# A macaron layer on one NeuronCore: the attention's output projection moved behind the heads, by two levels of seven products, with operands kept in DRAM

## The chip, the cores and the metric

The kernel runs on one core of one Trainium2 chip, in float32 throughout. The metric is the device time of one execution, in microseconds, of which the median over several runs is given. A profile of one execution is read beside it; its span runs from the first to the last instruction, and its own device time is a little more than the span.

## The reference

The input x has 1024 tokens (4 sequences of 256) of 512 numbers. Three blocks follow each other, each on the normalised x and added to x:

```python
x = x + 0.5 * _L0_ffn_ref(_layernorm(x), A, B, Wr)      # experts
x = x + _L0_attn_ref(_layernorm(x), wq, wkv, wo)        # 32 heads, causal
x = x + 0.5 * _L0_ffn_ref(_layernorm(x), A, B, Wr)      # the same experts again
```

The experts are 64 pairs of rank 16: h = x Aᵀ (512 to 1024), each h times its token's gate (softmax over the 16 largest of 64 scores), then h B (1024 to 512). The attention makes q, k and v of 128 numbers per head, softmax of the causal scores, and at the end multiplies the heads' outputs, 1024 tokens by 4096, with wo (4096 by 512). That last product is the output projection, and it is what changes place and form.

## The kernel before

**Seven products.** All large products go by Strassen's scheme in Winograd's form: a product of two 2×2 block matrices by 7 block products instead of 8, with sums of blocks ahead (`left_sums`, `right_sums`: four additions each) and seven additions of results behind. `seven` walks the products in the order M1, M2, M6, M5, M7, M3, M4; they share three PSUM banks, several products are added into one bank by TensorE, and each bank is read between two of them. For q, k and v two levels are nested (49 block products instead of 64): `xop` holds the 7×7 blocks of the normalised x, `two_levels` makes the 7×7 blocks of the weights on POOL, and `make_qk` and `v_stages` run one outer product or two at a time as a stage of seven inner ones.

**Order.** The heads are worked in 16 groups `p` of two. While group p attends, the q and k of group p+1 and a part of v are made. A group has 8 units, each a (head, sequence): `probs` (scores, mask, softmax) and, one unit later, `attend` (three transposes, then probabilities times v). The strings in `UNITS` (L994) say which step is taken between: q a q/k step, v a v step, o a step of the output projection, b the second half of `attend`. TensorE takes its instructions in the order a scheduler writes down[...].

**The output projection before.** It has one level and one group: K is two heads of 128, the tokens two halves of 512, the 512 outputs two halves of 256. `out_sums` makes three sums of 512 columns of the group's attention output (and one in place) on POOL, `sums_o` the four sums of wo's blocks on POOL, `project(p, u)` the seven products for a quarter of the tokens, each as two matmuls of 256 columns (L879), and reads the accumulators straight into x, seven times 512 columns (L891). The projection of group p-1 runs among the units of group p. For each group that is 28 matmuls and 14 reads.

**The second experts' layer** loads A and B again at the end and makes their block sums again on POOL (`load_experts(ctx, "f2", ...)`, L1057); it pairs token blocks t and t+4 (L1081).

**q and k.** For p > 0, `make_qk` runs four stages: (M1, M5), (M2, M6), (M7, M3), (M4), most of them two outer products wide, 512 columns; the parts are put together by adds on POOL (`done`, L711). `t3` and `t4` (L552, L555) turn weight block M1 into M7 and M2 into M4, in place, when the former use is over.

Of the kernel before, what the change touches and what calls it, by code (L numbers as in the profile page):

```python
# [13 lines left out]
P = 128  # L14
# [18 lines left out]
def macaron_kernel(  # L33
# [14 lines left out]
    small = ctx.enter_context(tc.tile_pool(name="small", bufs=4))  # L48
    xscope = ctx.enter_context(ExitStack())
# [30 lines left out]


    mask = const.tile([P, 3, P], F32, tag="mask", name="mask")
    nc.gpsimd.memset(mask, 0.0)
    for blk in (0, 2):
        nc.gpsimd.affine_select(
            out=mask[:, blk, :],
            in_=mask[:, blk, :],
            compare_op=ALU.is_ge,
            fill=MASKED,
            base=0,  # L90
            pattern=[[-1, P]],
            channel_multiplier=1,
        )
    mask_f = mask.rearrange("p b k -> p (b k)")

# [89 lines left out]
    def right_sums(eng, t, b11, b12, b21, b22, late=None, pinned=False):  # L185


        late = late or eng
        first = eng.tensor_tensor(b12, b12, b11, ALU.subtract)  # L189
        if pinned:  # L190
            tc.keep_in_program_order(first)
        eng.tensor_tensor(t[0], b22, b12, ALU.subtract)  # L192
        late.tensor_tensor(t[1], t[0], b11, ALU.subtract)
        late.tensor_tensor(t[2], b21, t[0], ALU.subtract)
        return {"M1": b11, "M2": b21, "M3": b22, "M4": t[2], "M5": b12, "M6": t[0], "M7": t[1]}
# [17 lines left out]
    def load_experts(scope, name, side, eng, between=None):  # L213
# [8 lines left out]
        a_v = a_t.rearrange("(c p) k -> p c k", p=P)  # L222
        b_v = b_t.rearrange("(c p) d -> p c d", p=P)

        def a_block(k, n):
            return slice(2 * k, 2 * k + 2), slice(512 * n, 512 * n + 512)

        def b_block(k, n):
            return slice(4 * k, 4 * k + 4), slice(256 * n, 256 * n + 256)

        for i, kn in enumerate(((0, 0), (1, 0), (1, 1), (0, 1))):
            c, e = a_block(*kn)
            nc.sync.dma_start(a_sb[:, c, e], a_v[:, c, e])
            if between is not None and i % 2:
                between(i // 2)
        for k in range(2):
# [4 lines left out]
        b_of = [b_sb[(slice(None), *b_block(*kn))] for kn in every]  # L241
        return (
            lambda: right_sums(eng, [at[:, i] for i in range(3)], *a_of, late=nc.gpsimd),
            lambda: right_sums(nc.gpsimd, [bt[:, i] for i in range(3)], *b_of),
        )

    def ffn(name, pairs, a_sums, b_sums, after, late, aside=None):


        with ExitStack() as scope:  # L250
# [165 lines left out]
            take(tokens, 1)  # L416
            if late:
                second = prepare(pairs[1])
                take(second, 1)
# [54 lines left out]
    OUTER = {"M1": 0, "M2": 1, "M7": 2, "M4": 3, "M5": 4, "M6": 5, "M3": 6}  # L474
    INNER = {"M1": 0, "M2": 1, "M7": 2, "M4": 3, "M5": 4, "M6": 5, "M3": 6}
    xop = xpool.tile([P, 7, 7, S], F32, tag="xop", name="xop")


    early = xop[:, 5:7, 6]

    def inner_sums(lo, hi, eng, between=None):
        o = slice(lo, hi)
        blocks = [xop[:, o, i] for i in range(4)]
        if lo == 0:
            blocks[2] = early
        left_sums(eng, [xop[:, o, i] for i in (4, 5, 6, 2)], *blocks, pinned=lo > 0, between=between)

    def last_outer():

        for of, i in ((early[:, 1], 2), (xop[:, 1, 3], 3)):  # L490
            tc.keep_in_program_order(
                nc.gpsimd.tensor_tensor(xop[:, 6, i], of, xop[:, 5, i], ALU.subtract)
            )

    def norm_pair(work, pair):
# [4 lines left out]
        where = [xop[:, k, 4:6, :].rearrange("p a s -> p (a s)") for k in (5, 6)]  # L500
        tokens = normed(work, pair, "a", where)
        yield
        for i, xn in enumerate(tokens):
            cols = slice(i * P, (i + 1) * P)
            pt = turned_x(xn, f"a_{pair[i]}").rearrange("p (o c) k -> p o c k", o=2)
            a11, a12, s3, a22, s1, s2, _ = (xop[:, k, sl, cols] for k in range(7))
            if half:
                nc.scalar.copy(a22, pt[:, 1])
                if a:
                    nc.vector.tensor_tensor(s3[:, 0], early[:, 0, cols], pt[:, 0, 0], ALU.subtract)  # L510
                    nc.vector.tensor_tensor(s3[:, 1], a11[:, 1], pt[:, 0, 1], ALU.subtract)
                else:
                    nc.vector.tensor_tensor(s3, a11, pt[:, 0], ALU.subtract)
                nc.vector.tensor_tensor(s2, pt[:, 1], s3, ALU.subtract)
                nc.vector.tensor_tensor(s1, a22, pt[:, 0], ALU.add)
            elif a:
                nc.scalar.copy(early[:, :, cols], pt[:, :, 0])
                nc.scalar.copy(xop[:, 0:2, 3, cols], pt[:, :, 1])
            else:
                nc.scalar.copy(xop[:, 0:2, sl, cols], pt)  # L520
        if half and not a:
            nc.vector.tensor_tensor(xop[:, 6, sl], xop[:, 1, sl], xop[:, 5, sl], ALU.subtract)
        elif a and not half:
            inner_sums(0, 2, nc.vector)

    raw, rights, outs, turns = {}, {}, {}, {}

    def load_o(p):

        w = opool.tile([P, HG, 512], F32, tag="w", name=f"wo_{p}")  # L530
        nc.sync.dma_start(w, wo_v[:, p * HG : (p + 1) * HG, :])
        raw["o", p] = w

    def sums_o(p):
        w = raw["o", p]
        t = opool.tile([P, 3, 256], F32, tag="t", name=f"to_{p}")
        b = [w[:, k, n * 256 : (n + 1) * 256] for k in range(2) for n in range(2)]
        rights["o", p] = right_sums(nc.gpsimd, [t[:, i, :] for i in range(3)], *b, pinned=p == 0)

    def two_levels(pool, bufs, name, blocks, pinned):  # L540
# [5 lines left out]
            for m in ("M1", "M5", "M2", "M3", "M6")  # L546
# [8 lines left out]
        def t4():  # L555
            return nc.gpsimd.tensor_tensor(t["M2"], t["M2"], t["M6"], ALU.subtract)

        def sums(pinned=pinned):
            plain = {m: v[:, 0:4] for m, v in t.items()}
            first = nc.gpsimd.tensor_tensor(plain["M5"], plain["M5"], plain["M1"], ALU.subtract)  # L560
            if pinned:
                tc.keep_in_program_order(first)
            nc.gpsimd.tensor_tensor(plain["M6"], plain["M3"], plain["M5"], ALU.subtract)
            right = {
                m: right_sums(
                    nc.gpsimd, [v[:, i] for i in range(4, 7)], *(v[:, i] for i in range(4))
                )
                for m, v in t.items()
            }
            right["M7"], right["M4"] = right["M1"], right["M2"]  # L570
            return right, t3, t4
# [3 lines left out]
    def load_qk(p):  # L575

        if p < NG:
            rights["qk", p] = two_levels(
                qkpool,
                6,  # L580
# [7 lines left out]
    def load_v(k):  # L588

        if 2 * k < NG:  # L590
            raw["v", k] = two_levels(
                vpool,
                5,
# [11 lines left out]
    with ExitStack() as scope:  # L605
# [7 lines left out]
            *experts,  # L613
# [4 lines left out]
        take(first_layer, 2)  # L618
# [7 lines left out]

    qkpool = right_pool(ctx, "wqk")
    hold = right_pool(ctx, "hold")
    opool = right_pool(ctx, "wo")
    attention = ExitStack()  # L630
    work = right_pool(attention, "work")
    pairs = right_pool(attention, "pairs")

# [8 lines left out]
    def make_qk(p):  # L642
        if p >= NG:
            return
        right, t3, t4 = rights["qk", p]
# [6 lines left out]
        def stage(ms, read, name):  # L652
            def product(n, ps, first):
                for i, m in enumerate(ms):
# [3 lines left out]
                        rhs=xop[:, OUTER[m], INNER[n]],  # L658
# [10 lines left out]
        def fresh(blocks):  # L669
            def read(r, ps):  # L670
                to = part(blocks, r)
                if READS[r][2]:
                    nc.vector.tensor_tensor(to, to, ps, ALU.add)
                else:
                    nc.scalar.copy(to, ps)
# [3 lines left out]
        def branch(blocks, into=None, of=slice(1, 2)):  # L679

            base = of

            def read(r, ps):
                to = part(blocks, r)
                of = to if READS[r][2] else part(base, r).to_broadcast(to.shape)
                nc.vector.tensor_tensor(to, of, ps, ALU.add)  # L686
                done(r, into)

            return read

        def onto(blocks, into=None):
            def read(r, ps):
                to = part(blocks, r)
                of = ps if ps.shape == to.shape else ps.to_broadcast(to.shape)
                nc.vector.tensor_tensor(to, to, of, ALU.add)  # L695
                done(r, into)

            return read

        def m47(r, ps):  # L700

            both, one, two, base = (part(slice(*k), r) for k in ((1, 3), (1, 2), (2, 3), (3, 4)))
            if READS[r][2]:
                nc.vector.tensor_tensor(both, both, ps, ALU.add)
            else:
                nc.scalar.copy(one, ps[:, 0:1])
                nc.vector.tensor_tensor(two, base, ps[:, 1:2], ALU.add)
            if r in LAST:
                nc.gpsimd.tensor_tensor(one, one, two, ALU.add)

        def done(r, into):  # L711

            if into is not None and r in LAST:
                to, a, b = (part(slice(k, k + 1), r) for k in (into, 1, 2))
                nc.gpsimd.tensor_tensor(to, a, b, ALU.add)  # L715


        if p > 0:
            yield from stage(("M1", "M5"), fresh(slice(1, 3)), "a")
            t3()  # L720
            yield from stage(("M2", "M6"), branch(slice(0, 2), 3), "b")
            t4()
        else:
            turns["qk"] = t3, t4

            yield from stage(("M1",), fresh(slice(3, 4)), "m")
            yield from stage(("M2",), branch(slice(0, 1), of=slice(3, 4)), "n")
            yield from stage(("M6",), onto(slice(3, 4)), "o")
            yield from stage(("M4", "M7"), m47, "r")
            yield from stage(("M5",), onto(slice(2, 4)), "s")  # L730
            load_qk(p + 1)
            yield from stage(("M3",), onto(slice(3, 4)), "u")
            return
# [389 lines left out]
```

## Time and profile before

| | us |
|---|---|
| median of 3 runs | 1177.11 (1176.92 to 1177.27) |
| the profiled execution's own time | 1176.84 |
| its span | 1175.1 |
| TensorE (PE) busy | 1162.9 |
| weight loads (PEld) busy | 1001.7 |
| VectorE (DVE) busy | 733.4 |
| POOL (GpSimd) busy | 681.5 |
| ScalarE (ACT) busy | 490.8 |
| moved by DMA | 47.46 MB |

Busy times are sums over the span. A matmul's record is longer than its share of the engine, since matmuls overlap: pace is read from the starts of successive rows. A float32 matmul leaves two records, so a count of 8 records is four matmuls. The transposes leave one.

### The profile page before, as it was taken

The numbers are of one execution on the slowest core, as the hardware profiler recorded it, in microseconds if no ns is written. First come the engines' busy times: TensorE is split into PE (matmuls) and PEld (weight loads), VectorE is DVE, ScalarE is ACT, GpSimd is POOL, SyncE is SP. The second block draws the span as 40 slices with busy tenths as digits, with TensorE's granted clock in tenths as the row PEclk, the third lists the DMA queues.
The fourth block names the chain that finished last, engine by engine and source line by source line (L and its number), as shares of the span: only waits on it lengthen the run. The fifth ranks groups of instructions, "written<-read, shape, count | busy, mean of one in ns | idle before, by whom it ended". The sixth has DMA issues, their size and how long they took to land.

```text
span 1175.1 us, 18545 instructions
## 1 busy us (share of the span) xinstructions
PE 1162.9 (99%) x6492; PEld 1001.7 (85%) x6492; DVE 733.4 (62%) x1927; ACT 490.8 (42%) x1365; POOL 681.5 (58%) x942
## 2 busy tenths in 40 slices
PE   8999999999999999999999999999999999999998
PEld 5677889999999989898989898989898988875767
DVE  5544775566656665666576667666666666675432
ACT  4344234434443444344434444434444344546420
POOL 4615497975757575766667575856675644451110
PEclk9999999999999999999999999999999999999999
DMA  7001121111011111111111102011111000400001
GB/s 255 1 1 36 45 64 28 37 36 46 19 45 37 46 27 37 37 45 30 35 46 37 46 19 63 22 43 37 45 28 36 19 28 1 162 1 1 18 18 36
DMA packets 64940, 47.46 MB, mean 40 GB/s; under 512 B 4432, under 2 KB 55632, under 8 KB 64848
## 3 DMA queue, kind: packets, MB, share of 16 engines
q1 hardware_dynamic: 64848, 46.28, 13.4%
q8 instruction: 51, 0.84, 0.3%
q14 instruction: 41, 0.34, 0.1%
HBM read 44.17 MB, written 2.10 MB: 39 GB/s over the span
## 4 chain that ended last, share of the span: by engine, by line
PE 96%; DVE 1%; ACT 1%; DMA 1%; SPq 0%; issue 0%; DVEq 0%; ACTq 0%
PE po L879 16%; PE po_f L395 8%; PE pqk_a L655 8%; PE pqk_c L655 8%; PE pqk_b L655 8%; PE ph_f L327 8%; PE ps L902 5%; PE pa L947 5%; PE pv_c L763 4%; PE pqk_d L655 4%; PE pv_b L763 4%; PE ptp L942 4%; PE ps L901 2%; PE pa L954 2%; PE pv_e L763 2%; PE pv_d L763 2%
## 5 line engine op out<-in xcount | busy, mean ns | idle before, releaser
L891 DVE TENSOR_TENSOR x<-x,po 128x512 f32<-128x512 f32 x224 | 153.9, 688 | 73.6 <-PE po L879 71.5
L944 ACT COPY pT<-ptp 128x384 f32<-128x384 f32 x128 | 61.3, 479 | 211.5 <-PE ptp L942 211.5
L921 ACT ACTIVATE s<-s,least 128x128 f32<-128x128 f32 (+1 forms) x256 | 114.4, 447 | 75.0 <-DVE least L910 75.0
L931 ACT ACTIVATE s<-s,arden 128x128 f32<-128x128 f32 (+1 forms) x256 | 102.5, 448 | 50.5 <-DVE arden L929 50.1
L715 POOL TENSOR_TENSOR qk<-qk 128x256 f32<-128x256 f32 x120 | 87.1, 728 | 57.9 <-DVE qk L686 28.5
L910 DVE CUSTOM_DVE_ANT_0 s<-ps,mask 128x128 f32<-128x128 f32 (+1 forms) x256 | 81.4, 356 | 50.5 <-PE ps L902 50.4
L357 POOL TENSOR_TENSOR hg_f<-hg_f,gate_f 128x512 f32<-128x512 f32 x32 | 33.5, 1059 | 128.8 <-DVE hg_f L340 68.9
L655 PE MATMUL pqk_a<-xop,wqk_M 128*128 128x256 f32 x420 | 107.9, 380 | 0.0
L655 PE MATMUL pqk_c<-xop,wqk_M 128*128 128x256 f32 x420 | 107.1, 380 | 0.0
L655 PE MATMUL pqk_b<-xop,wqk_M 128*128 128x256 f32 x420 | 106.5, 380 | 0.0
L695 DVE TENSOR_TENSOR qk<-qk,pqk_c 128x512 f32<-128x512 f32 x105 | 72.2, 688 | 41.0 <-PE pqk_c L655 32.0
L686 DVE TENSOR_TENSOR qk<-qk,pqk_b 128x512 f32<-128x512 f32 x105 | 72.2, 687 | 25.6 <-PE pqk_b L655 25.2
L189 POOL TENSOR_TENSOR wo<-wo 128x256 f32<-128x256 f32 x16 | 11.7, 729 | 126.9 <-DMA wo<-in_wo 126.9
L961 ACT COPY attn<-pa 128x256 f32<-128x256 f32 x128 | 47.6, 372 | 89.0 <-PE pa L954 88.9
L655 PEld LDWEIGHTS pqk_c<-xop,wqk_M 128*128 128x128 f32 x420 | 76.1, 190 | 8.6 <-DVE qk L695 0.3
L655 PEld LDWEIGHTS pqk_b<-xop,wqk_M 128*128 128x128 f32 x420 | 73.2, 191 | 6.3
L655 PEld LDWEIGHTS pqk_a<-xop,wqk_M 128*128 128x128 f32 x420 | 72.5, 191 | 6.2 <-POOL wqk_M L192 0.3
L902 PE MATMUL ps<-qk 128*128 128x256 f32 x256 | 76.5, 380 | 0.0
L947 PE MATMUL pa<-pT,vbuf 128*128 128x256 f32 x256 | 76.2, 379 | 0.0
L879 PE MATMUL po<-wo,so 128*128 128x256 f32 x256 | 66.7, 383 | 1.8 <-DVE so L180 1.8
L879 PE MATMUL po<-to,attn 128*128 128x256 f32 x256 | 66.2, 381 | 0.9 <-DVE x L891 0.9
L879 PE MATMUL po<-wo,attn 128*128 128x256 f32 x256 | 64.7, 379 | 0.0
(199 smaller groups left out, 2806.6 us busy)
## 6 DMA issues: line engine op xcount, KB each, us to landing
wv_M<-in_wkv SPq DMA_DIRECT2D x64, 128.0 KB, 2.6
wqk_M<-in_wq SPq DMA_DIRECT2D x64, 128.0 KB, 2.3
wqk_M<-in_wkv SPq DMA_DIRECT2D x64, 128.0 KB, 2.5
wo<-in_wo SPq DMA_DIRECT2D x16, 512.0 KB, 3.9
a_f<-in_a_t SPq DMA_DIRECT2D x8, 512.0 KB, 6.1
b_f<-in_b_t SPq DMA_DIRECT2D x4, 1024.0 KB, 9.6
x<-in_x SPq DMA_DIRECT2D x8, 256.0 KB, 7.6
out_x<-x SPq DMA_DIRECT2D x16, 128.0 KB, 1.7
```

The source lines that it names most:

```text
L327: nc.tensor.matmul(ps, lhsT=left[m][:, c, :], rhs=a_right[m][:, c, :], start=first and c == 0, stop=c == 1, skip_group_check=True,)
L395: nc.tensor.matmul(ps[:, 0:256], lhsT=left[m][:, c, :], rhs=b_right[m][:, c, :], start=first and c == 0, stop=c == 3, skip_group_check=True,)
L655: nc.tensor.matmul(ps[:, i * S : (i + 1) * S], lhsT=right[m][n], rhs=xop[:, OUTER[m], INNER[n]], start=first and i == 0, stop=True, skip_g ...
L715: nc.gpsimd.tensor_tensor(to, a, b, ALU.add)
L763: nc.tensor.matmul(ps[:, i * S + t * P : i * S + (t + 1) * P], lhsT=xop[:, OUTER[m], INNER[n], t * P : (t + 1) * P], rhs=right[m][n], star ...
L879: nc.tensor.matmul(ps[:, tt * 256 : (tt + 1) * 256], lhsT=outs[p][m][:, (2 * u + tt) * P : (2 * u + tt + 1) * P], rhs=right[m], start=firs ...
L891: nc.vector.tensor_tensor(to, to, ps.rearrange("p (t d) -> p t d", t=2), ALU.add)
L902: nc.tensor.matmul(ps[:, P : 3 * P], lhsT=qT[:, P : 2 * P], rhs=kT, start=True, stop=True)
L910: nc.vector.tensor_tensor_reduce(out=s[:, cols], in0=ps[:, cols], in1=mask_f[:, cols], scale=-SCALE, scalar=-TAKEN, op0=ALU.add, op1=ALU.m ...
L921: nc.scalar.activation(s[:, cols], s[:, cols], AF.Exp, bias=least[:, i : i + 1], scale=-1.0, accum_out=den[:, i : i + 1],)
L931: nc.scalar.mul(s[:, cols], s[:, cols], rden[:, i : i + 1])
L947: nc.tensor.matmul(po[:, 0 : 2 * P], lhsT=v_of(p, j, 2 * b), rhs=pT[:, 0 : 2 * P], start=True, stop=False,)
```

## The change

**What is computed.** The whole output projection becomes one product, 1024 by 4096 by 512, by two levels. Outer blocks: two halves of the tokens, the even and the odd head of each group as the two halves of K, two halves of the outputs. Inner blocks: halves of these again (256 tokens, 128 outputs; K by whether the pair of groups' first or second is meant). There are 7 outer products, each in 4 steps along K, each step 2×7 inner products of two matmuls of 128 columns: 7 × 4 × 28 = 784 matmuls. A step's results are accumulated in four PSUM banks over the four steps of an outer product; only then are they read, into `y` and from there into x.

**Where its operands come from.** Behind each group its four attention blocks and three sums go to DRAM (`sum_left`, `kept_left`: 7 × 512 columns per group), and wo's sums likewise (`sum_right`, `kept_right`). The step's operands are loaded back (`load`, four DMAs of 2 × 512 KB and 2 × 256 KB) into three rotating buffers and one extra, and the inner sums are made on VectorE (`sums`, eight additions per step).

**What moves with it.** The experts' sums of the first layer are written to DRAM and loaded for the second (`keep`, `load_kept`) instead of being made again. M4 of the q, k and v weights gets a buffer of its own (7 and 6 buffers instead of 6 and 5), is made ahead, and `t4` goes. q and k take five stages: M1, (M2, M6), (M4, M7), M5, M3, as v does. `xop` becomes seven tiles, the mask moves into a pool that ends with the heads, the second experts' layer pairs t and t+1, and all unit strings are new. In the last group the projection's steps stand among the units; the rest follows behind.

```diff
+    def load_kept(pool, of, m):
+        ...
+        to = pool.tile(shape, F32, tag=f"{of}_{m}", name=f"{of}_f2_{m}", bufs=1)
+        if m in A_GIVEN:
+            c, e = block(*A_GIVEN[m])
+            nc.sync.dma_start(to, view[:, c, e])
+        else:
+            nc.sync.dma_start(to, kept[:, A_AT[m]])
 ...
-            for m in ("M1", "M5", "M2", "M3", "M6")
+            for m in ("M1", "M5", "M2", "M3", "M6", "M4")
 ...
-        def t4():
-            return nc.gpsimd.tensor_tensor(t["M2"], t["M2"], t["M6"], ALU.subtract)
+            inner("M1")
+            inner("M2")
+            nc.gpsimd.tensor_tensor(t["M6"][:, 0:4], t["M3"][:, 0:4], t["M5"][:, 0:4], ALU.subtract)
+            inner("M6")
+            for m in ("M5", "M3"):
+                inner(m)
+            nc.gpsimd.tensor_tensor(t["M4"], t["M2"], t["M6"], ALU.subtract)
 ...
-            yield from stage(("M1", "M5"), fresh(slice(1, 3)), "a")
-            t3()
-            yield from stage(("M2", "M6"), branch(slice(0, 2), 3), "b")
-            t4()
-        yield from stage(("M7", "M3"), onto(slice(1, 4, 2), 2), "c")
-        load_qk(p + 1)
-        yield from stage(("M4",), onto(slice(1, 2)), "d")
+        yield from stage(("M1",), m1, "a")
+        if p > 0:
+            t3()
+            yield from stage(("M2", "M6"), onto_copy(slice(0, 4, 3)), "b")
+        ...
+        yield from stage(("M4", "M7"), m47, "c")
+        yield from stage(("M5",), onto(slice(2, 4)), "d")
+        load_qk(p + 1)
+        yield from stage(("M3",), onto(base), "e")
 ...
+    def sum_left(p):
+        s = hold.tile([P, 3, 512], F32, tag="so", name=f"so_{p}", bufs=1)
+        blocks = attns[p].rearrange("p j (h t) -> p (j h) t", h=2)
+        to = kept_left[p // 4][:, p % 4]
+        ...
+        eng = nc.vector if p == NG - 1 else nc.gpsimd
+        left_sums(eng, [s[:, i] for i in range(3)], *(blocks[:, k] for k in (0, 2, 1, 3)))
+        def keep():
+            ...
+                nc.sync.dma_start(to[:, 0:4], blocks)
+            nc.sync.dma_start(to[:, 4:7], s)
+        return keep
 ...
+        def load(k):
+            m, of = OUT_ORDER[k // 4], k % 4
+            pool, n = (outer["pool"], 1) if k > 6 and k % 4 == 3 else (stream, 3)
+            left = pool.tile([P, 2, 7, S], F32, tag="l", name=f"ol_{m}_{of}", bufs=n)
+            right = pool.tile([P, 2, 7, P], F32, tag="r", name=f"or_{m}_{of}", bufs=n)
+            for g in range(2):
+                ...
 ...
+        for k in range(steps):
+            for ahead in range(2 + (k > 4), 3 + (k > 3)):
+                if k + ahead < steps:
+                    load(k + ahead)
+            if k % 4 == 0:
+                banks = accumulators(k)
+            left, right = operands.pop(k)
+            summing = sums(k + 1) if k + 1 < steps else iter(())
+            for i in range(14):
+                g, (n, at) = i // 7, (IN_ORDER[i % 7], i % 7)
+                if 2 <= i < 10:
+                    take(summing, 1)
+                if i % 2 == 0:
+                    take(reading, 1)
+                for t in range(2):
+                    cols = at % 2 * 256 + t * P
+                    nc.tensor.matmul(
+                        banks[at // 2][:, cols : cols + P],
+                        lhsT=left[n][:, g, t * P : (t + 1) * P],
+                        rhs=right[n][:, g],
+                        ...
+                yield
+            take(summing, 1)
+            if k % 4 == 3:
+                take(reading, 100)
+                reading = read(OUT_ORDER[k // 4], banks)
 ...
-    second_layer = ffn("f2", [(t, t + 4) for t in range(4)], *experts, after=store, late=False)
-    next(second_layer)
-    take(projecting[1], 7)
+    for step in range(done, 8 * 7 * 7):
+        if step == 55:
+            keep()
+            attention.close()
+            outer["pool"] = right_pool(ctx, "outer")
+        ...
+        if step in (8 * 7 * 5 + 36, 8 * 7 * 6 + 20):
+            next(second_layer)
+        take(projecting, 1)
```

`read` (new) takes an outer product's seven inner results out of the four banks: one copy on ScalarE, seven additions of 256 columns on VectorE into `y`, and then one to three additions of 1024 columns from `y` into x or into a running sum.

## The prediction

> **What bounds the kernel now.** First the page's busy times and its 40 slices:
>
> ```profile
> PE 1162.9 (99%) x6492; PEld 1001.7 (85%) x6492; DVE 733.4 (62%) x1927; ACT 490.8 (42%) x1365; POOL 681.5 (58%) x942
> ...
> PE   8999999999999999999999999999999999999998
> ...
> PEclk9999999999999999999999999999999999999999
> ```
>
> TensorE is busy in every slice at full clock. Because matmuls overlap, I check this in the chain of waits: 96% of it is PE. And in the busy times of one stretch of two groups of heads:
>
> ```profile
> 443.60:558.40 114.80, 114.80 (x683) 104.17 (x682) 75.53 (x187) 48.84 (x144) 75.38 (x108) 1.00 0.14 38
> ```
>
> In order: length, then PE, PEld, DVE, ACT, POOL busy, clock, DMA share, GB/s. PE never pauses; DVE and POOL work two thirds of the time. So time falls only by fewer or shorter matmuls, and it is lost wherever another engine makes PE wait. What a matmul costs is read from starts, in the timeline of PE:
>
> ```profile
> 213.70 1.05 PE L763 MATMUL pv_b<-wv_M,xop 128*128 128x128 f32 x8
> 214.59 1.03 PE L655 MATMUL pqk_a<-xop,wqk_M 128*128 128x256 f32 x4
> 215.46 1.05 PE L763 MATMUL pv_b<-wv_M,xop 128*128 128x128 f32 x8
> ```
>
> Two records are one matmul. Four of 128 columns take 0.89 (213.70 to 214.59), two of 256 take 0.865 (several such pairs): **0.2225 and 0.4325 us** each. As a test: a group has 49 q/k, 28 projection and 16 attention matmuls of 256 columns, 49 + 16 of 128, and 24 transposes at 0.11: 40.2 + 14.5 + 2.6 = 57.3 us, twice that 114.6 against the stretch's 114.8. The rows carry the sum.
>
> **1. The products of the projection.** Removed: 28 matmuls of 256 columns in 16 groups, 448 × 0.4325 = 193.8 us. Added: 784 of 128 columns × 0.2225 = 174.4 us. All stand on PE, the bound: **-19.3 us**. No other matmul changes in number: q/k still has 49 per group.
>
> A rule speaks against this. The Trainium skill ("TensorE: Matmul & The Clock Gate", Back-to-back issue gap) says that in a stream where each matmul has its own weight load, 128 columns sustain about 81 ns instead of 56, 1.45 times the isolated pace. At 1.45 × half of 0.4325 a matmul of 128 columns would cost 0.31 us, 784 of them 246 us, and the change would lose 52 us. But the pv rows above are just that case, 128 columns with a new weight load each, and they cost 0.2225, 3% over half of 256 columns. I take the row.
>
> **2. VectorE in the output phase.** Four of the 28 steps run among the last group's heads; 24 stand behind, 28 × 0.2225 = 6.23 us of PE each. A step needs four additions of 512 and four of 256. Rows: 0.69 and 0.42 long; but starts show less:
>
> ```profile
> 1161.27 0.68 DVE L382 TENSOR_TENSOR hgT_f<-pth_f,hgT_f 128x512 f32<-128x512 f32 x1
> 1161.87 0.68 DVE L384 TENSOR_TENSOR hs_f<-pth_f,hs_f 128x512 f32<-128x512 f32 x1
> 1162.47 0.41 DVE L407 TENSOR_TENSOR x<-x,po_f 128x256 f32<-128x256 f32 x1
> ```
>
> 0.60 apart, so 0.60 × 4 + 0.34 × 4 = 3.8 us (4.4 by durations). Every fourth step adds a read: seven additions of 256 (2.9) and one to three of 1024 (1.2 each by at_f's row, L192). Four steps: 15.0 to 17.7, + 2.9, + 1.9 on average, so 20 to 22.5 of PE's 24.9 us. VectorE fits, but the step behind a boundary carries 3.8 + 0.4 + up to 3.6 = 7.8 against 6.2. The sums are issued a step ahead and first needed by the third inner product, which covers most of this. Six boundaries, from 0 to 2 us each: 0 to 12; I take **+2**, nearest to the row of spacing.
>
> The second rule: the skill ("GPSIMD Engine Reference", Key points) says that POOL shares its SBUF interfaces with VectorE and collides with VectorE's instructions of two SBUF inputs. The trace shows it once:
>
> ```profile
> 1040.33 2.35 POOL L194 TENSOR_TENSOR bt_f<-b_f,bt_f 128x1024 f32<-128x1024 f32 x1
> ...
> 1040.54 2.42 DVE L180 TENSOR_TENSOR so<-attn 128x256 f32<-128x256 f32 x1 [0.44 <-ACT attn L961]
> ```
>
> An addition of 0.42 took 2.42, until POOL's was over. All 224 new sums are of this kind. At 2 us a hit the rule would cost hundreds of us, if POOL worked beside them; but the change leaves POOL idle in that phase (the second experts' layer's eight sums of 2.36 are not made again). Only the last group's start has both: POOL's four sums of the group before, 4 × 1.27 = 5.1 us.
>
> **3. The operands from DRAM.** A step loads 1.5 MiB, 1.57 MB, rows of 2 KB and 1 KB, in 6.23 us: 252 GB/s. The trace's fastest loads:
>
> ```profile
> 8.00:12.00 4.00, 3.97 (x25) 2.77 (x23) 2.92 (x11) 0.90 (x2) 0.00 (x0) 1.00 1.03 384
> 20.00:24.00 4.00, 4.00 (x11) 1.75 (x10) 1.95 (x5) 0.58 (x1) 3.92 (x3) 1.00 1.04 280
> ```
>
> 384 GB/s with the experts' and x's rows of 2 KB; 280 in a window with rows of 512 bytes. So 4.1 to 5.6 us per step, loaded two to three steps ahead: hidden, **0** (without the cover, at 200 GB/s, +1.6 × 24 = 38 us). Storing costs 2.4 MB per group of some 45 us, 53 GB/s beside the 38 moved now: hidden. On SP's queue the stores wait for POOL's sums with weight loads behind them, but those are wanted some 10 us later; lateness there appears in 4. The second layer's b, 3.7 MB, can be loaded only when the stream's buffers are free: 9.5 us, wanted after 14 matmuls of 512 columns (0.86 each: six ph_f records take 2.58 in the chain), 12 us: hidden. Storing the first layer's sums, 4.2 MB, holds SP until POOL has made them, some 40 us before the next weights are used: 0.
>
> **4. The groups of heads.** PE per two groups falls to 114.8 - 2 × 12.1 = 90.6. DVE loses 14 × 0.69 per group and gains a stage of q/k (17.5 us instead of 14.6 by rows): 62 of 90.6. POOL loses four adds of 0.73 per group: about 70 of 90.6, 77% instead of 66. The tight place is POOL's chain to `t3`. M6's tile takes the buffer that stage e of the group before frees at its end. Behind that stand, in the changed order, in every second group: M6 1.27, eight sums for M6 and M5 3.65, M3's four 1.82, three adds to v 2.19, M4 2.09, v's four 1.82, the four sums of attention 5.1, then t3 2.09: **20.0 us**. PE reaches the first use of t3's result after 21 q/k matmuls (9.1), 22 of v (4.9), 4 scores (2.6), 4 × 3 transposes (1.3), 3 × probabilities times v (2.0) and the M4 half (0.4): **20.3 us**. In the other groups 18.1 against 22.1. So the change lives on a margin of 0.3 us in seven groups. What queues behind a late t3 on PE is everything: the attention too. Bounds: 0 to 2 us in each of seven groups, 0 to 14; I take **+2**, since spacing is a little below duration here too.
>
> **5. Entry and exit.** In the last group's first three units no projection stands between the attention's instructions; softmax's latency (DVE, ACT twice, DVE between) is bare for about three units, and the first sums wait for the first load and collide with POOL as in 2. 0 to 10; **+2**. The load itself is early, since `xop` is given back tile by tile. At the exit the last read holds the PSUM banks that the second layer's first products want: two or three additions, +1 to 5; **+2**. In exchange the old handover goes: in 1018 to 1055.6 PE is busy 34.9 of 37.6: **-2.7**, for what is late next there is now among the +4. The first 180 us: M4 is made earlier on POOL, two adds of 2.09 ahead, but the x sums behind are reached earlier by as much: 0, from -2 to +2.
>
> **Sum.** 1175.1 - 19.3 + 2 + 2 + 2 + 2 - 2.7 = 1161.1 of span. Outside it lie 1.7 us (1176.84 - 1175.1), and the median lies 0.3 over the profiled run: **1163 us**, 1.2% faster.
>
> **Rivals.**
> - *VectorE becomes the bound of the output phase.* For it: 20 to 22.5 of 24.9 us, unevenly. Against: sums are a step ahead. If every boundary costs its surplus and the slots behind it, 2 us × 6, and the entry 5: 1163 + 10 + 3 = **1176**, hardly better than before; half of it, **1170**.
> - *POOL's chain decides: slower.* Place: t3 in each group. Price: one us of lateness is one us of PE. With stores, loads and v's reads in the chain, 20.0 can become 23; two us in each of 15 groups is 30: 1163 - 2 + 30 = **1191**. It decides from about 1.1 us per group on (16 us of gain over 15 groups). For it: the margin; POOL waits in the trace for DMA and PE already (18 and 8 us before L560 and L563). Against: the chain's rows are steady (729 or 456 ns each) and the other half of the groups has 4 us.
> - *The stream of operands falls behind:* at 200 GB/s **1201**. Against: 384 shown for the same rows; not shown with stores to and loads from the same DRAM tiles.
> - *Weight loads bind at 128 columns*, the rule in 1: **1215**. The pv rows speak against it.
> - *It doesn't do what it says:* the changed order holds all 784 products and none of the old 448; excluded.
>
> **How the numbers follow.** Forecast as above (1156 to 1168): 0.60. VectorE or entry and exit dearer, 1168 to 1175: 0.21. Within 0.2% of before, about what a measurement of this kernel tells from no change (1174.8 to 1179.5): 0.04. POOL's chain: 0.09; the stream: 0.04; weight loads: 0.02. Faster 0.81, same 0.04, slower 0.15. The low end is no loss at all but the exit's 1, 1175.1 - 19.3 - 2.7 + 1 + 2 = 1156; the high end, 1176, leaves out the slow cases.
>
> **What would show it.** Right: 784 matmuls of 128 columns, each 0.22 us after the last; two groups of heads in 90.6 to 92 us; steps of 6.2 us; DMA at about 250 GB/s there. Wrong: PE waiting for POOL at stage c (4), for VectorE's sums at a step's third product (2), for DMA at a step's first (3), or steps of 8 us with PE never idle (1).

## The result, and the profile after

The changed kernel takes **1158.83 us** (median of 4 runs, 1158.39 to 1159.82) against 1177.19 (4 runs, 1176.92 to 1178.39) before: ratio **0.9843**, 95% interval 0.9826 to 0.9860. The profiled execution takes 1158.9 us with a span of 1157.1, 18.0 less than before. The page of the changed kernel, its busy times and three rows of its 40 slices:

```profile
PE 1147.0 (99%) x7164; PEld 1009.6 (87%) x7164; DVE 756.9 (65%) x2096; ACT 483.5 (42%) x1438; POOL 617.0 (53%) x866
...
PE   9999999999999999999999999999999999999998
...
PEclk9999999999999999999999999999999999999999
DMA  9101111213233142233233232322386998741001
```

TensorE is still the bound and never gives up a tenth; its busy time fell by 15.9 us. What is new stands in the last row: six to nine tenths of the DMA capacity in six slices towards the end, where the operands stream in. The busy times of four stretches, in the same columns as before the change (length, PE, PEld, DVE, ACT, POOL, clock, DMA share, GB/s): two groups of heads, the entry of the output phase, its long middle, and the first 20 us of the second experts' layer.

```profile
497.40:588.40 91.00, 91.00 (x570) 83.17 (x569) 61.49 (x174) 47.34 (x152) 69.79 (x101) 1.00 0.30 100
843.40:857.00 13.60, 11.86 (x77) 10.10 (x75) 9.30 (x32) 10.57 (x35) 5.45 (x4) 1.00 0.98 309
905.00:1024.00 119.00, 119.00 (x1069) 119.00 (x1068) 102.13 (x212) 5.68 (x13) 0.00 (x0) 1.00 0.87 292
1040.20:1060.00 19.80, 19.80 (x78) 11.13 (x77) 13.74 (x65) 11.81 (x24) 4.23 (x4) 1.00 0.29 111
```

Only the entry has a pause (1.74 us). In the middle VectorE is busy 102 of 119 us and the DMA engines 87%, and PE loses nothing. The pace of the new products is read in the chain of waits, whose longest link is this (start, length, records; two records are one matmul):

```profile
902.81 120.46 PE po_M L1063 x1076
```

538 matmuls in 120.46 us: **0.2239 us** each. Where the 18.0 us come from, by landmarks (work that stands in both of PE's timelines): products -18.4 (784 × 0.2237 = 175.4 against 193.8); two groups take 90.94 instead of the 90.56 that the counts give at that pace, 7 × 0.37 = +2.6; entry +1.7; one late load in the seventh step of the projection +0.4; the old handover -2.7; start -1.0; exit -0.5. That sums to -17.9.

### The profile page after: what moved, and what is told of

It reads as the page before. It is cut to its first block, busy times and chain, and to the rows that moved or that the text cites. A ratio compares the mean times of both kernels' runs of the same rounds, so it can differ in the third digit from the quotient of the medians.

```text
span 1157.1 us, 20441 instructions
## 1 busy us (share of the span) xinstructions
PE 1147.0 (99%) x7164; PEld 1009.6 (87%) x7164; DVE 756.9 (65%) x2096; ACT 483.5 (42%) x1438; POOL 617.0 (53%) x866
## 4 chain that ended last, share of the span: by engine, by line
PE 95%; DVE 2%; DMA 1%; ACT 1%; issue 0%; SPq 0%; DVEq 0%; ACTq 0%
PE po_M L1063 14%; PE pqk_c L714 8%; PE po_f L418 8%; PE ph_f L350 8%; PE pqk_b L714 8%; PE pa L1130 5%; PE ps L1085 5%; PE pqk_e L714 4%; PE pqk_d L714 4%; PE pv_c L808 4%; PE pqk_a L714 4%; PE pv_b L808 4%; PE ptp L1125 4%; PE pa L1137 2%; PE ps L1084 2%; PE pv_e L808 2%
## 5 line engine op out<-in xcount | busy, mean ns | idle before, releaser
L1063 PE MATMUL po_M<-or_M,ol_M 128*128 128x128 f32 x1568 | 178.6, 275 | 1.4 <-DVE or_M L975 1.3
L1063 PEld LDWEIGHTS po_M<-or_M,ol_M 128*128 128x128 f32 x1568 | 177.0, 192 | 2.1 <-DVE or_M L975 1.9
L187 POOL TENSOR_TENSOR wqk_M<-wqk_M 128x128 f32<-128x128 f32 x320 | 137.9, 456 | 9.7
L714 PE MATMUL pqk_c<-xop,wqk_M 128*128 128x256 f32 x448 | 114.4, 380 | 0.1
L975 DVE TENSOR_TENSOR ol_M<-ol_M 128x512 f32<-128x512 f32 x112 | 77.7, 694 | 21.5 <-DMA ol_M<-left 19.6
L731 DVE TENSOR_TENSOR qk<-qk,pqk_c 128x256 f32<-128x256 f32 (+1 forms) x112 | 59.6, 532 | 42.0 <-PE pqk_c L714 24.9
L731 DVE TENSOR_TENSOR qk<-qk,pqk_d 128x512 f32<-128x512 f32 x112 | 74.7, 684 | 11.8 <-PE pqk_d L714 8.1
L187 POOL TENSOR_TENSOR wv_M<-wv_M 128x128 f32<-128x128 f32 x160 | 69.0, 456 | 11.2 <-DMA wv_M<-in_wkv 4.8
L430 DVE TENSOR_TENSOR x<-x,po_f 128x256 f32<-128x256 f32 x56 | 23.5, 420 | 63.4 <-PE po_f L418 63.3
L714 PE MATMUL pqk_a<-xop,wqk_M 128*128 128x256 f32 x224 | 64.2, 381 | 0.5 <-ACT qk L738 0.5
```

Of the source, the lines that this page charges most:

```text
L187: pieces = [lambda eng, of=of: eng.tensor_tensor(*of, ALU.subtract) for of in sums]
L714: nc.tensor.matmul(ps[:, i * S : (i + 1) * S], lhsT=right[m][n], rhs=xop[OUTER[m]][:, INNER[n]], start=first and i == 0, stop=True, skip_g ...
L1063: nc.tensor.matmul(banks[at // 2][:, cols : cols + P], lhsT=left[n][:, g, t * P : (t + 1) * P], rhs=right[n][:, g], start=k % 4 == 0 and g ...
```

## The experiments

"Against the change" below is the difference to the kernel before, measured beside it, set against the changed kernel's own difference of -18.4 us. The intervals of the ratios are about ±0.0013, that is ±1.6 us, and ±2.0 for the changed kernel; a difference below some 2.5 us is therefore not told by the times, and is read from the traces.

| kernel | us, median (runs) | ratio to before, 95% | against the change |
|---|---|---|---|
| one level | 1176.45 (12) | 1.0000 [0.9992, 1.0009] | +18.3 |
| no inner sums | 1157.33 (4) | 0.9837 [0.9824, 0.9851] | -0.8 |
| right sums on POOL | 1163.08 (4) | 0.9888 [0.9874, 0.9901] | +4.9 |
| 256 columns | 1153.79 (5) | 0.9807 [0.9794, 0.9820] | -4.4 |
| t3 later | 1164.02 (4) | 0.9896 [0.9881, 0.9911] | +6.0 |
| few reads | 1160.90 (4) | 0.9873 [0.9857, 0.9890] | +2.8 |
| half the products | 1133.19 (1) | single run | -24.9 |
| half, no sums | 1105.76 (1) | single run | -52.3 |
| three strings | 1158.48 (5) | 0.9847 [0.9834, 0.9860] | +0.5 |
| POOL's sums later | 1159.09 (4) | 0.9855 [0.9842, 0.9869] | +1.1 |
| both | 1159.40 (4) | 0.9855 [0.9841, 0.9868] | +1.4 |
| strings to 13, sums on VectorE | 1155.87 (5) | 0.9827 [0.9814, 0.9840] | -2.0 |

### Is it the second level?

```diff
-                nc.vector.tensor_tensor(of[to], of[a], of[b], op)   # the inner sums
-                for t in range(2):
+                for tile_of in {0: (0,), 1: (1, 2), 2: (3,), 3: (4, 5), 4: (6,), 5: (7,), 6: ()}[at]:
+                    r, t = divmod(tile_of, 4)
                     nc.tensor.matmul(
-                        banks[at // 2][:, cols : cols + P],
-                        lhsT=left[n][:, g, t * P : (t + 1) * P],
-                        rhs=right[n][:, g],
+                        banks[t // 2][:, t % 2 * 256 : t % 2 * 256 + 256],
+                        lhsT=left[:, g, 2 * r + t // 2, t % 2 * P : (t % 2 + 1) * P],
+                        rhs=right[:, g, 2 * r : 2 * r + 2].rearrange("p n d -> p (n d)"),
```

> The projection stays where the change put it, with the same operands from DRAM, but has one level only: no inner sums, 16 matmuls of 256 columns per step (448 in all, 0.4325 us each) instead of 28 of 128, and two copies on ScalarE instead of the inner read. Theory (the second level is the whole gain; place, stream and storing cost next to nothing): PE gets back 193.8 - 175.4 = 18.4 us, so about 1177 us, the time before within 2 us. Rival A (the gain is from moving the projection out of the units, or from fewer reads on VectorE): close to the changed kernel, 1158 to 1165. Rival B (move and stream cost something that the second level paid for): above 1179.

Measured 1176.45 against 1176.52 before: no difference, within 0.1%. The chain of this kernel has the long link in matmuls of 256 columns:

```profile
890.19 149.36 PE po_M L1042 x692
```

346 matmuls at 0.4317 us. So the move to the end, the fewer reads on VectorE and 89 MB more of DMA traffic (136.6 against 47.5) come to nothing together: what they cost and what they bring cancel. **The second level is the whole gain.** Both rivals of this run fall.

### Does VectorE hold the phase up?

```diff
-                nc.vector.tensor_tensor(of[to], of[a], of[b], op)
                 yield
             operands[k] = (...)      # M3 to M7 take blocks as loaded
```

> Leaves out the 224 inner sums of the operands on VectorE (products use blocks as loaded), and nothing else; matmuls, loads and reads stay. Theory (VectorE's sums are hidden beside 6.27 us of PE per step): 0 to -1.5 us, all of it at the entry of the last group. Rival (VectorE holds the output phase up at the six boundaries, as the +2 of the forecast or the VectorE rival had it): -3 to -12 us.

0.8 us faster by the ratios, 1.5 by the medians. The profile says where. The 20 us around the entry, first the changed kernel, then the one without sums:

```profile
840.00:860.00 20.00, 18.26 (x121) 16.08 (x120) 15.55 (x50) 13.54 (x45) 7.24 (x7) 1.00 0.89 293
```

```profile
840.00:860.00 20.00, 19.55 (x134) 17.57 (x133) 9.30 (x38) 12.18 (x40) 7.29 (x8) 1.00 0.87 277
```

PE is busy 1.29 us more here. From the start of the first product to that of the last it takes 185.62 us instead of 187.62; of these 2.00, 1.55 are the pause at the entry and the slower matmul behind it, and some 0.4 a wait in the seventh step. (The first steady group of heads starts 0.6 us later in this execution, which hides a part of it in the time.) From the eighth step on the starts keep the same distance within 0.01 us, through five of the six boundaries: these cost nothing. 224 additions, 106.4 us of VectorE's busy time (756.9 against 650.5), lie beside PE but for these two places.

How much room is left, two kernels show that halve PE's work:

```diff
-                for t in range(2):
+                for t in range(2) if g == 0 else ():
```

> Leaves out the second half along K (g = 1) of every step's products: 392 matmuls of 128 columns instead of 784; loads, sums and reads stay. If TensorE's pace alone set the output phase: 1158.8 - 392 x 0.2237 = 1071 us. But a step's 3.1 us of PE is then less than VectorE's 5.0 to 5.6 us and than the loads' 4.1 to 5.6 us: 24 steps behind the heads at 5.0 to 5.6 us instead of 6.26, about 1128 to 1143 us. What it comes to is the second bound of the phase, the room that the kernel still has.

> As the kernel with half the products, and also without the 224 inner sums on VectorE: only loads (1.57 MB per step), half of the products and the reads stay. If VectorE held that kernel up, this one is faster by the difference, down to the loads' own pace: at 384 GB/s 4.1 us per step, about 1107 us; at 280 GB/s 5.6 us, about 1143 us. If the loads held it up, both take the same time within 3 us.

The same 55 us of the phase in the two kernels, with sums and without:

```profile
905.00:960.00 55.00, 37.72 (x284) 35.78 (x283) 51.03 (x106) 0.75 (x2) 0.00 (x0) 0.94 1.06 376
```

```profile
905.00:960.00 55.00, 38.41 (x308) 36.77 (x308) 16.13 (x31) 4.02 (x10) 0.00 (x0) 0.97 1.06 376
```

With sums VectorE is busy 51 of 55 us, and every pause of PE ends with one of its sums; in the timeline of PE 15 steps start between 905.81 and 988.48, **5.5 us** each. Without sums the chain goes from load to load:

```profile
935.33 8.90 DMA ol_M<-left
944.24 8.28 DMA or_M<-in_wo
952.54 9.01 DMA ol_M<-left
961.57 8.27 DMA or_M<-right
```

A link of the chain is the time from a load's issue to its landing. Eight steps start between 921.51 and 960.22, **4.8 us** each, at 376 GB/s; the second layer's weights are loaded in the same time, so a step's own 1.57 MB take 4.2. A step is thus bounded by PE at 6.27 us, by VectorE at 5.5, by the loads at 4.8. The first kernel's time lies in the expected range; the second's is 1 us below the 1107 of the faster rate (4.1 us per step), though its steps took 4.8: that is luck. The expectations had left out that the four steps among the heads get shorter too: together they take 36.3 us in the changed kernel, 27.5 with half the products, 25.7 without the sums as well.

### Weight loads, and 256 columns

```diff
-                for t in range(2):
-                    ... lhsT=left[n][:, g, t * P : (t + 1) * P], rhs=right[n][:, g]
+                ... lhsT=right[n][:, g], rhs=left[n][:, g]          # 256 columns
```

> The roles of the two operands are exchanged in the projection's products: one matmul of 256 columns (weights: right block, 128 columns; moving: left block, 256 columns) instead of two of 128 with two weight loads. The 392 results lie transposed in the banks and are added to x so, without being turned back: that part of the computation is changed. Durations of the trace (0.4325 against 2 x 0.2237): 392 x 0.0149 = -5.8 us. The skill's rule (a stream of 128-column products with their own weight loads runs 1.45 times slower than its columns): 128-column products should lose 0.09 us each against 256 columns, so -60 us or more.

The long link of its chain:

```profile
888.23 130.63 PE po_M L1062 x604
```

302 matmuls at 0.4326 us, against 2 × 0.2239: 0.0152 less, times 392 is 6.0 us; 4.4 by the ratios and 5.0 by the medians were measured. From the first product to the last PE takes 181.52 us instead of 187.62, 6.1 less; in this execution the first steady group of heads starts 1.0 us later, which takes back the rest. Splitting 256 columns into two matmuls with two weight loads costs 3.5%, not the 45% that the rule in step 1 of the prediction would make of it.

### POOL beside VectorE

```diff
-                nc.vector.tensor_tensor(of[to], of[a], of[b], op)
+                (nc.gpsimd if of is r else nc.vector).tensor_tensor(of[to], of[a], of[b], op)
```

> The four right sums of 256 columns of each step go to POOL, which is otherwise idle behind the heads; the four left sums stay on VectorE. The skill's rule of the shared interfaces (an addition of 0.42 us took 2.42 us once) would have each of VectorE's four sums of two SBUF inputs stretched by up to 2 us where it meets one of POOL: 24 steps with 2.8 us on VectorE becoming 5 to 9 us, steps of 6.3 us then limited by it in part: +10 to +60 us. If the collision stretches only the one or two that meet (some 1 us per step): VectorE has 2 us of room per step, 0 to +3 us.

+4.9 us: between the two expectations, nearer the small one. In the trace POOL's sums of 256 columns take 0.72 to 1.70 us (median 1.06), and VectorE's of 512 columns beside them 1.13 in the median instead of 0.69. Behind 908 us the steps keep the changed kernel's pace all the same: the room in each step absorbs this. What is lost is lost before, most of it in one pause and what follows it, in PE's timeline (the pause in brackets) and in the clock one microsecond later:

```profile
858.21 8.38 PE L1063 MATMUL po_M<-or_M,ol_M 128*128 128x128 f32 x60 [2.44 <-POOL or_M L975]
```

```profile
859.00:860.00 1.00, 1.00 (x7) 1.00 (x6) 0.33 (x4) 0.69 (x3) 1.00 (x3) 0.50 1.01 410
```

PE waited 2.44 us, then ran at half clock for some 3 us: the 30 matmuls took 8.21 us to the next row instead of 6.7. From start to start this entry costs 2.6 us more than the changed kernel's, and two waits for VectorE's sums in the seventh step (0.89 and 0.36 us) 1.3 more: 3.9 between the first product and the last. The pause isn't the price of collisions alone, since POOL's first right sum starts only at 855.86, behind its four sums of the group before; how it divides is not shown.

### Is t3 the tight place?

```diff
         def t3():
+            for _ in range(2 if name.startswith("wqk") else 0):
+                nc.gpsimd.tensor_tensor(t["M1"], t["M6"], t["M1"], ALU.subtract)
             return nc.gpsimd.tensor_tensor(t["M1"], t["M6"], t["M1"], ALU.subtract)
```

> Two more additions of 128x896 (2.09 us each, taking back and forth, so t3's result stays) stand on POOL right ahead of t3 in each group of q and k from 1 to 15: t3's result is 4.2 us later. The forecast's count (20.0 us of POOL against 20.3 of PE, 0.3 us of room in every second group, 4 in the others): 3.9 us lost in seven groups and 0.2 in the others, +25 to +30 us. What the trace of the changed kernel shows (t3 done at 545.4, first used at 552.4: 7 us of room in the one kind of group, 8 in the other): 0, at most +3 us where the delayed additions behind t3 are wanted.

Neither: +6.0 (5.2 by the medians). First, the changed kernel's own timeline, POOL and then PE, in a group in which I had seen no room:

```profile
524.13 1.27 POOL L605 TENSOR_TENSOR wqk_M<-wqk_M,wqk_M 128x512 f32<-128x512 f32 x1
...
543.34 2.09 POOL L588 TENSOR_TENSOR wqk_M<-wqk_M,wqk_M 128x896 f32<-128x896 f32 x1
```

```profile
552.37 1.03 PE L714 MATMUL pqk_c<-xop,wqk_M 128*128 128x256 f32 x4
```

M6 (L605) to the end of t3 (L588) is 21.3 us, close to my 20.0; but it begins at 524.1, while stage e runs until 532.7. So it doesn't wait for the buffer that stage e frees, and t3's result lies ready for 7 us. With t3 4.2 us later, who waits? VectorE and then PE, between 200 and 840 us and 224 and 815 (us in total, times, longest):

```profile
DVE qk L733 <- POOL qk L767: 3.0, 6, 0.6
```

```profile
PE pqk_d L716 <- DVE qk L733: 2.4, 6, 0.5
```

In the changed kernel the first of these is 0.3 in one place. It is not t3 that is wanted but the additions to q and k that POOL makes *behind* it (`m47`, L765): VectorE's read in stage d needs them, and PE needs the bank. That costs 0.5 to 0.7 us per pair of groups, 3.8 in all. Another 2.4 us are lost before the first pair. Of these, 1.0 come from the two additions, which stand in group 0 as well, as my expectation had left out; the other 1.4 are there before the first of them runs (the first q/k product starts at 129.04 instead of 127.67), so they are scatter of the start. The additions thus cost 4.9 us. POOL's room comes to some 3.6 us, an estimate (4.2 of delay less 0.6 of loss), at another place than I said.

### Where two groups lose 0.37 us

```diff
             def read(r, ps):
+                if p > 0 and r not in LAST:
+                    return
```

> Leaves out, for groups of q and k from 1 on, VectorE's reads of the accumulators of the single-product stages M5 and M3, all but the last four of each; all products stay. Theory (the two groups' 91.0 us instead of 90.6 come from these reads, because a stage of one product per step comes back to a bank before VectorE has read it): -2 to -3 us, two groups in 90.5 us. Rival (the loss is elsewhere, or the count by 0.2225 us is that much too small): 0 to -0.7 us, two groups still in 90.9 us.

A miss, and no clean test: leaving reads out also moved some of TensorE's steps, since their order is made from what stands around them. Weight loads wait for VectorE's reads for 8.6 us in the changed kernel between 170 and 845 us, mostly in 0.2 us that the overlap hides. With few reads, between 224 and 815:

```profile
PEld pa L1132 <- ACT pT L1129: 1.9, 7, 0.3
PEld pqk_d L714 <- DVE qk L731: 1.7, 7, 0.2
```

The wait at stage e is gone, a new one of 0.3 per pair stands at the probabilities (seven times), and a pair takes 91.12. I then read the changed kernel's lateness row by row, start against start, in seven pairs: 0.09 us at stage d, 0.14 at stage e, 0.17 around the probabilities times v behind it, always at the same three places. Three strings put v steps there:

```diff
-            "qqvbqqvbqqv",
-            "qqqbqqvbqv",
+            "qqvbvqqbqqv",
+            "qqbqqvqbqv",
         ...
-            "qqvbqqqbvq",
+            "qqvbqqvbqq",
```

> Only the order of steps changes in three strings of the units, at the three places where the trace of the changed kernel shows TensorE late in each pair of groups: 0.09 us at stage d and 0.14 at stage e (a product waits for VectorE's read of its bank), 0.17 around probabilities times v of the unit behind (waits for ScalarE's copy of the transposed probabilities). v steps are put between. Theory (these three make the 91.0 instead of 90.6 us): two groups in 90.5 to 90.6 us, -2 to -2.8 us in all. Rival (the rest is the pace of the matmuls themselves, or the wait only moves to another place, as when reads were left out): two groups stay at 90.9 or go above, 0 to +2 us.

Two groups of this kernel:

```profile
498.00:588.60 90.60, 90.60 (x570) 82.95 (x569) 61.49 (x174) 47.17 (x152) 69.73 (x101) 1.00 0.30 99
```

90.60, as expected, and as the prediction had it. Yet the time stayed (+0.5): the same strings serve group 14, which has no v left to put between, and PE pauses there (0.41 and 0.33 us at 848 to 850) and in the last group's projection (0.59 at 904). In the profiled execution, the slowest of the five, the start is 1.3 us later too.

### The entry

```diff
-            if unit == 0 and p > 0:
+            if unit == 1 and last:
+                take(keep_first(p - 1), 1)
+            if unit == 2 * last and p > 0:
                 keep = sum_left(p - 1)
-            if unit == 2 - last and p > 0:
+            if unit == 2 + 2 * last and p > 0:
                 keep()
```

> In the last group POOL's four sums of group 14 are made two units later (its first block is stored ahead, since a step wants it early). In the changed kernel they ran at 850.2 to 855.7 beside VectorE's first sums of operands, two of which took 1.57 and 1.28 us instead of 0.69 and 0.42, and TensorE waited 1.29 us right there. Theory (the collision makes the wait of the entry): -1 to -1.5 us, the pause at 855.7 gone, and VectorE's stretched sums now some units later, where a step's cover hides them. Rival (the first sums are late because softmax stands before them, not by the collision): 0 to -0.4 us, or more where the later stores hold loads up.

> The three strings and POOL's later sums together. If both theories hold: the sum of the two, -3 to -4 us against the changed kernel, about 1155 us. If one falls, the value of the other alone.

Neither kernel gains, but the first edit did not do what I meant: POOL has nothing else to do, and its four sums ran at 850.6 to 856.2 as before, with VectorE's two additions at 1.57 and 1.28 us again. The collision was therefore untested. In the last kernel VectorE makes them:

```diff
-        eng = nc.vector if p == NG - 1 else nc.gpsimd
+        eng = nc.vector if p >= NG - 2 else nc.gpsimd
         ...
+            if p == NG - 2:
+                here = UNITS[0][:6] + ("qqvbqqvbqqv", "qqqbqqvbqv")
         ...
-            if unit == 0 and p > 0:
+            if unit == 1 and last:
+                take(keep_first(p - 1), 1)
+            if unit == 4 * last and p > 0:
                 keep = sum_left(p - 1)
-            if unit == 2 - last and p > 0:
+            if unit == 2 + 4 * last and p > 0:
                 keep()
```

with the new strings up to group 13. The sums and their store also stand later in the program, as before; VectorE makes them at 848.9 to 852.0 all the same.

> Two edits, each read from its own stretch of the trace. The three new strings now only up to group 13; group 14, which has no v steps left to put between, keeps its old ones. Group 14's four sums go to VectorE, so that POOL does nothing when the first operands are summed (putting them later in the program had left them at the same time, since POOL had nothing else). Theory (strings were right and only hurt group 14; the collision makes the pause at the entry): two groups in 90.6 us again, 6 x 0.33 = -2.0 us, and no stretched sum and less than 0.5 us of pause between 853 and 858, -0.8 to -1.3 us; with the scatter of the start about 1156 us, the fastest of all. Rival (the four sums cost VectorE 2.4 us just where softmax needs it, so the pause stays): the entry as before or worse, 1157 us. If the strings cost elsewhere too: 1158 to 1159 us.

**1155.87 us**, 2.0 less than the change by the ratios and 3.0 by the medians; the two intervals overlap, so the gain stands on the two traces. In the last kernel PE takes 1.7 us less from the first product to the last (185.88 against 187.62), and two groups of heads take 90.60 again; its start is 0.6 us later. POOL, VectorE and PE at the entry, in the changed kernel:

```profile
852.76 1.27 POOL L167 TENSOR_TENSOR attn<-attn 128x512 f32<-128x512 f32 x1
853.99 1.72 POOL L167 TENSOR_TENSOR so<-attn,so 128x512 f32<-128x512 f32 x1
```

```profile
853.01 1.57 DVE L975 TENSOR_TENSOR ol_M<-ol_M 128x512 f32<-128x512 f32 x1
...
854.71 1.28 DVE L975 TENSOR_TENSOR or_M<-or_M 128x256 f32<-128x256 f32 x1
```

```profile
856.98 7.86 PE L1063 MATMUL po_M<-or_M,ol_M 128*128 128x128 f32 x68 [1.29 <-DVE or_M L975]
```

and in the last one:

```profile
851.97 0.67 DVE L975 TENSOR_TENSOR ol_M<-ol_M 128x512 f32<-128x512 f32 x1
...
852.79 0.42 DVE L975 TENSOR_TENSOR or_M<-or_M 128x256 f32<-128x256 f32 x1
```

```profile
854.25 7.82 PE L1063 MATMUL po_M<-or_M,ol_M 128*128 128x128 f32 x68
```

The same first additions take 0.67 and 0.42 instead of 1.57 and 1.28, though VectorE had four sums more just ahead, and the pause is gone. In the changed kernel each of the two runs beside an addition of POOL and ends only after it (854.58 after 854.03, 855.99 after 855.71). The order in which VectorE now works is not the reason: counted from PE's first products of the projection (852.33 and 851.05), VectorE starts the first addition after 0.68 us in the changed kernel and after 0.92 in the last one. The stretch of the two rows, 1.76 us, is enough for all of the 1.29.

## Why the prediction was right

1163 was said, 1158.83 came, inside the likeliest case's own range (1156 to 1168). By its steps:

1. **Products, -19.3: right.** Measured -18.4, since a matmul of 128 columns keeps 0.2237 to 0.2239 us over hundreds instead of the 0.2225 of four. With one level the gain is 0; with 256 columns 3.5% are got back, not the 45% of the rule. The row of the trace was to be trusted over the rule's pace.
2. **VectorE's boundaries, +2: mechanism right, term mis-sized.** 102 of 119 us busy is 21.4 per four steps, within the 20 to 22.5; but five of the six boundaries cost nothing, because the sums are made a step ahead. Some 0.4 is lost behind the first one, where a load is late as well (3). The collision with POOL was rightly put at the last group's start alone: two rows stretched by 1.76 us, one pause of 1.29.
3. **Stream, 0: right.** 292 GB/s in the middle, 376 when nothing else binds. One wait shows that the queue's order matters: for the seventh step VectorE waits for a load that stands in SP's queue behind the last group's stores. SP's queue waits 7.3 us there for ScalarE, which copies that group's attention output; the load is issued at 892.54 and lands 6.69 us later,

```profile
899.33 0.69 DVE L975 TENSOR_TENSOR ol_M<-ol_M 128x512 f32<-128x512 f32 x1 [5.20 <-DMA ol_M<-left]
```

   and PE loses some 0.4 us there, from start to start: the cover held all but this.
4. **Groups, +2: the number held (+2.6) by luck, the reason failed.** "The change lives on a margin of 0.3 us" was wrong: I let M6 wait for stage e's buffer, and it starts 8.6 us sooner. No group loses anything at t3. What is lost are three small pauses where a step of one product comes back to a bank, or to the probabilities, too soon now that the projection's steps have left the units: with v steps put at these three places two groups take 90.60. The chance given to POOL's chain (0.09) rested on that step.
5. **Entry +2: +1.7, right in place and cause. Exit +2: -0.5;** the second layer's first products start without a pause. Old handover -2.7: gone as read. The first 180 us, 0: -1.0, but the first steady group starts anywhere from 224.5 to 225.9 us in kernels that don't touch the start, so this may all be scatter.

The sum was 4 us too high: the exit (by 2.5), the boundaries (1.6), the start (1.0) and the entry (0.3) were put too high, the products (0.9) and the groups (0.6) too low. That these misses cancel in part is luck; that the products carry the forecast is not.

## What to carry to other kernels

Where one engine is busy in every slice, count its instructions by the spacing of their starts and let that carry the forecast; a cover of a whole step (operands made one step ahead, loaded two or three ahead) was worth its face value here, and a reserve for each boundary only biased the sum. Before calling a chain tight, look in the trace for what really releases its first link; a length alone says nothing. And work taken out of the steady loop also took away what stood between two dependent steps: re-read the fillers there, group by group, and in the last groups separately.

## What the hardware showed beyond that

A pause of 2.44 us on TensorE was followed by 3 us at a granted clock of 0.50, while a pause of 1.29 us left it at 1.00. In the kernel with half the products two pauses of 2.79 us each went before 14 matmuls: the one lot took 3.39 us, the other 5.02. A pause of 2.29 us there was followed by some 6 us at 0.50; one of 2.66 had ended 3.4 us before it. The length of one pause alone doesn't decide it. An addition of two SBUF operands on VectorE took 1.57 instead of 0.69 us beside an equal one on POOL. With a stream of such additions on each of the two engines all through the phase, those of VectorE took 1.13 us in the median. Loads of 256 and 512 KB with rows of 1 and 2 KB held 376 GB/s over 55 us.
